# Blocks of tokens behind a branch on their count, in two routed layers

## The chip, the cores and the metric

The kernel runs on one core of one Trainium2 chip (trn2). A core has TensorE for matrix products (its weight loads are shown as an engine of their own, PEld), VectorE (DVE), ScalarE (ACT), GpSimd (POOL) and SyncE (SP), each with an instruction queue of its own, and DMA engines that move data between the chip's main memory and the core's SBUF. TensorE writes into PSUM. The metric is the device time of one execution in microseconds (us); lower is better.

## The reference

One network of four layers runs over 16 batches of 64 tokens with 256 features, x of shape (16, 64, 256), and over a context of 16 x 1024 rows. Each layer is a cross attention, a mixing step and a feed-forward part, each added to x. Two of the feed-forward parts matter here; both are routed: a router gives every token to one or two of eight experts.

```python
# layer 0: two experts of eight per token, and a shared expert
scores = jax.nn.softmax(xt @ gate_w.T, axis=-1)
topk_w, topk_i = jax.lax.top_k(scores, 2)
comb = jnp.zeros((T, E)).at[jnp.arange(T)[:, None], topk_i].add(topk_w)
for e in range(E):
    y = y + comb[:, e:e + 1] * _swiglu(xt, w1[e], w2[e], w3[e])
# layer 1: one expert of eight per token
gates = one_hot(argmax(probs)) * probs
h = relu(einsum('bsd,edf->besf', x, W1) + b1)
y = einsum('besf,efd->besd', h, W2) + b2
out = einsum('bse,besd->bsd', gates, y)
```

There are 1024 tokens, so 2048 assignments in layer 0 and 1024 in layer 1. The hidden width is 704 in layer 0 (`silu(t @ w1) * (t @ w3) @ w2`) and 1024 in layer 1. How many tokens an expert gets is known only once the router has run.

## The kernel before, in words

The kernel computes only the assigned tokens. It writes the normalized tokens to a buffer `hs` in main memory, ranks them within their experts, and cuts every expert's list into blocks of 128. With eight experts, 2048 assignments fill at most 16 + 7 = 23 blocks and 1024 at most 8 + 7 = 15; these are `L0_BLOCKS` and `L1_BLOCKS`. The program always runs that many. A block that is past the last one in use takes the last expert's weights and some of its tokens again; its result is written to rows that nobody reads.

`blocks` (from line 1232 on) makes the tables for it on VectorE: `nb`, the blocks of each expert, `end`, their running sum, and from these, for every block, the rows of the weights (`rows`) and the rows of the tokens (`tokens`). It is a chain of some 25 small operations with one small matrix product in it.

For each block j, GpSimd issues three gathers by indirect DMA (`gather_rows`, line 1280): the first weights into `wa`, the second weights into `wb`, the tokens into `hb`. Each has three buffers, so the gathers run up to three blocks ahead of the products. TensorE transposes the tokens (line 179), VectorE or ScalarE in turn copies them to SBUF as `dT` (`evict`, lines 60 and 62: a switch flips at each call when the program is written out), TensorE multiplies with `wa` into PSUM (`gu` in layer 0, `ph` in layer 1, line 67), ScalarE and VectorE apply the activation and write `hid`, and TensorE multiplies `hid` with `wb` into `po`. ScalarE copies `po` to `yb` (line 1303) and issues its write to the buffer `ys` on its own DMA queue (line 1304). The next layer begins with `carry`, which gathers from `ys` by the tokens' places and adds to x.

In layer 0, `L0_ffn` first runs the second half of the shared expert (`shared_part`, lines 1150 to 1169), which uses a tile `hid` of its own with two buffers, while `blocks` runs and the first gathers are on their way. In layer 1, `L1_ffn` adds the experts' second bias by eight small products in the same place.

The order of the work within a layer is found by a planner of the framework from priorities (the order in which the program is written) and modelled times; it may bring an operation forward past others. Some layers fix TensorE's order by hand; the two routed layers don't. The weights of other layers are brought in by SP into a ring of two slots.

Of the kernel before, what the change touches and what calls it, by code (L numbers as in the profile page):

```python
# [11 lines left out]
F32 = mybir.dt.float32  # L12
I32 = mybir.dt.int32
# [6 lines left out]
B, S, D = 16, 64, 256  # L20
# [4 lines left out]
NK = KEYS // 128  # L25
E = 8
L0_BLOCKS = 2 * T // 128 + E - 1
L1_BLOCKS = T // 128 + E - 1
CAP = 160
L2_CUTS = ((0, 128), (128, CAP - 128))  # L30
RING = 7296
# [5 lines left out]
CHUNK = 256  # L37
# [3 lines left out]
class Net:  # L41
# [1098 lines left out]
            nc.vector.tensor_tensor(g, p, m, ALU.mult)  # L1140
            self.over_experts(g, ALU.add, "", r.gates[x][:, tiles])

    def L0_block(self, j):
        w = self.lp.tile([128, 4 * 704], F32, tag="wa", bufs=3, name="wa")
        self.gather_rows(w, self.a["L0f_w13"], self.rows[:, j : j + 1])
        w2 = self.lp.tile([128, 6 * D], F32, tag="wb", bufs=3, name="wb")
        self.gather_rows(w2, self.a["L0f_w2r"], self.rows[:, j : j + 1])
        return w.rearrange("p (u c f) -> p u c f", u=2, c=2), w2.rearrange("p (m f) -> p m f", f=D)

    def shared_part(self, k):  # L1150

        nc = self.nc
        w1, w3, w2 = self.shared
        cols = bass.ts(k, CHUNK)
        hid = self.lp.tile([128, 3, CHUNK], F32, tag="hid", bufs=2, name="hid")
        for m in range(3):
            at = slice(m * 128, m * 128 + 128)
            ps = self.lps.tile([128, 2, CHUNK], F32, tag=self.tag, bufs=self.tag_bufs, name="gu")
            for u, w in enumerate((w1, w3)):
                self.mm(ps[:, u, :], [(w[:, c, at], self.hT[:, c, cols]) for c in range(2)])  # L1160
            g = self.lp.tile([128, CHUNK], F32, tag="g", bufs=2, name="g")
            nc.scalar.activation(g, ps[:, 0, :], AF.Silu)
            nc.vector.tensor_tensor(hid[:, m, :], g, ps[:, 1, :], ALU.mult)
            yield
        for t in range(2):
            po = self.misc([128, D])
            self.mm(po, [(hid[:, m, t * 128 : (t + 1) * 128], w2[:, m, :]) for m in range(3)])
            self.add_to_x(2 * k + t, po)
            yield

    def L0_ffn(self):
        nc = self.nc
        self.rows, self.tokens = self.blocks(self.routed, L0_BLOCKS)
        self.tag, self.tag_bufs = "gu", 4
        for k in range(2, NC):
            for _ in self.shared_part(k):
                pass
        self.start_pack(self.at)
        sizes = [128] * 5 + [64]
        for j in range(L0_BLOCKS):  # L1180
            w13, w2 = self.L0_block(j)
            dT = self.block_tokens(j)
            hid = self.lp.tile([128, 6, 128], F32, tag="hid1", bufs=2, name="hid1")
            for m2 in range(3):
                ps = self.lps.tile([128, 2, 2, 128], F32, tag="gu", bufs=4, name="gu")
                for v in range(2):
                    m = m2 * 2 + v
                    n = sizes[m]
                    for u in range(2):
                        self.mm(  # L1190
                            ps[:n, u, v, :], [(w13[:, u, c, m * 128 : m * 128 + n], dT[:, c, :]) for c in range(2)]
                        )

                for lo, v, n in ((0, 2, 128),) if m2 < 2 else ((0, 1, 128), (1, 1, 64)):
                    g = self.lp.tile([128, 2, 128], F32, tag="g1", bufs=3, name="g1")
                    nc.scalar.activation(g[:n, :v, :], ps[:n, 0, lo : lo + v, :], AF.Silu)
                    nc.vector.tensor_tensor(
                        hid[:n, m2 * 2 + lo : m2 * 2 + lo + v, :], g[:n, :v, :], ps[:n, 1, lo : lo + v, :], ALU.mult
                    )
            po = self.lps.tile([128, D], F32, tag="o", bufs=2, name="po")  # L1200
            self.mm(po, [(hid[:n, m, :], w2[:n, m, :]) for m, n in enumerate(sizes)])
            self.block_out(j, po)

# [25 lines left out]
    def blocks(self, r, n_blocks):  # L1232


        nc = self.nc
        ps = self.misc([128, E])
        self.mm(ps, [(self.ones, r.seen)])

        nb = self.lp.tile([128, E], F32, name="nb")
        nc.vector.tensor_scalar(nb, ps, 127.0, 1.0 / 128, ALU.add, ALU.mult)  # L1240
        nc.vector.tensor_scalar(nb, nb, 0.49609375, 12582912.0, ALU.subtract, ALU.add)
        nc.vector.tensor_scalar(nb, nb, 12582912.0, None, ALU.subtract)
        end = self.lp.tile([128, E], F32, name="end")
        nc.vector.tensor_tensor_scan(end, self.ones[:, :E], nb, 0.0, ALU.mult, ALU.add)
        shape = [128, n_blocks, E]
        past = self.lp.tile(shape, F32, name="past")
        nc.vector.tensor_tensor(
            past, self.steps[:, :n_blocks].unsqueeze(2).to_broadcast(shape),
            end.unsqueeze(1).to_broadcast(shape), ALU.is_ge,
        )  # L1250
        of = self.lp.tile([128, n_blocks], F32, name="of")
        nc.vector.tensor_reduce(of, past, AX.X, ALU.add)
        nc.vector.tensor_scalar(of, of, E - 1.0, 128.0, ALU.min, ALU.mult)
        rows = self.lp.tile([128, n_blocks], I32, name="rows")
        nc.vector.tensor_scalar(rows, of, self.lane, None, ALU.add)

        nc.vector.tensor_tensor(past, past, end.unsqueeze(1).to_broadcast(shape), ALU.mult)
        at = self.lp.tile([128, n_blocks], F32, name="at_block")
        nc.vector.tensor_reduce(at, past, AX.X, ALU.max)
        nc.vector.tensor_tensor(at, self.steps[:, :n_blocks], at, ALU.subtract)  # L1260
        nc.vector.tensor_scalar(at, at, T / 128 - 1.0, None, ALU.min)
        nc.vector.scalar_tensor_tensor(at, of, T / 128 / 128, at, ALU.mult, ALU.add)
        nc.vector.tensor_scalar(at, at, self.lane, None, ALU.is_equal)
        ps = self.misc([128, n_blocks])
        self.mm(ps, [(r.table, at[: E * T // 128])])
        tokens = self.lp.tile([128, n_blocks], I32, name="tokens")
        nc.vector.tensor_copy(tokens, ps)
        first = self.lp.tile([128, E], F32, name="first")
        nc.vector.tensor_tensor(first, end, nb, ALU.subtract)
        nc.vector.tensor_scalar(first, first, 128.0, 1.0, ALU.mult, ALU.subtract)  # L1270
        for m, to in zip(r.masks, r.at):
            t = self.gate("back_t")
            nc.vector.tensor_tensor(t, r.place, first.unsqueeze(1).to_broadcast([128, NT, E]), ALU.add)
            nc.vector.tensor_tensor(t, t, m, ALU.mult)
            slot, _ = self.over_experts(t, ALU.add, "back_r")
            nc.vector.tensor_copy(to, slot)
        return rows, tokens

    def gather_rows(self, out, src, at):
        return self.nc.gpsimd.indirect_dma_start(out, None, src, bass.IndirectOffsetOnAxis(ap=at, axis=0))  # L1280

# [8 lines left out]
                self.xs[:, i, :], y, g[:, i : i + 1], self.xs[:, i, :], ALU.mult, ALU.add  # L1290
            )

    def block_tokens(self, j):

        hb = self.lp.tile([128, D], F32, tag="hb", bufs=3, name="hb")
        self.gather_rows(hb, self.hs, self.tokens[:, j : j + 1])
        dT = self.lp.tile([128, 2, 128], F32, tag="dT", bufs=2, name="dT")
        self.evict(dT, self.transposed(hb))
        return dT
# [10 lines left out]
        self.nc.sync.dma_start(b2, self.a["L1f_b2"])  # L1310
        return w, row, b2

    def L1_block(self, j):
        w = self.lp.tile([128, 2 * 1024 + 8], F32, tag="wa", bufs=3, name="wa")
        self.gather_rows(w, self.a["L1f_W1b"], self.rows[:, j : j + 1])
        w2 = self.lp.tile([128, 8 * D], F32, tag="wb", bufs=3, name="wb")
        self.gather_rows(w2, self.a["L1f_W2r"], self.rows[:, j : j + 1])
        return (
            w[:, : 2 * 1024].rearrange("p (c f) -> p c f", f=1024), w[:, 2 * 1024 :],
            w2.rearrange("p (m f) -> p m f", f=D),  # L1320
        )

    def L1_ffn(self):
        nc = self.nc
# [9 lines left out]
        for i in range(NT):  # L1334
# [4 lines left out]
            po = self.misc([128, D])  # L1339
            self.mm(po, [(gT, b2)])  # L1340
            self.add_to_x(i, po)
        for j in range(L1_BLOCKS):
            w1, b1, w2 = self.L1_block(j)
            dT = self.block_tokens(j)
            hid = self.lp.tile([128, 8, 128], F32, tag="hid", bufs=2, name="hid")
            for m4 in range(2):
                ph = self.lps.tile([128, 4, 128], F32, tag="h", bufs=3, name="ph")
# [9 lines left out]
            po = self.lps.tile([128, D], F32, tag="o", bufs=2, name="po")  # L1357
            self.mm(po, [(hid[:, m, :], w2[:, m, :]) for m in range(8)])
            self.block_out(j, po)

    def pack_L2_gate(self):
        self.slot()
# [900 lines left out]
```

## Time and profile before

| | us |
|---|---|
| median of 3 runs | 3081.01 |
| lowest and highest run | 3073.53, 3089.68 |
| the profiled execution | 3078.14 |
| its span | 3076.4 |
| blocks of layer 0, first to last result | 301.69 to 503.96 |
| blocks of layer 1, first to last result | 1240.46 to 1347.93 |

The page and the answers of the trace give times from the span's start. A row of the timeline reads: start, duration, engine, line, operation, what it writes and reads, the tile's shape, how many are merged in the row (xN), and in brackets how long the engine had been idle before it and what ended that. A row of the waits reads: who waited for whom, the sum, how many times, the longest. A row of the stretches reads: the stretch, its length, and each engine's busy time with its number of instructions, then the granted TensorE clock, the busy share of the DMA engines and what they moved. The DMA rows read: queue, packets, MB, share of 16 engines' time.

### The profile page before, as it was taken

The page shows a single profiled execution, that of the slowest core. Times are in us where ns is not written, and L with a number is a line of the kernel's source. Part 1 is how long each engine was busy: PE and PEld are TensorE (multiplying, and loading weights), DVE is VectorE, ACT ScalarE, POOL GpSimd, SP SyncE. Part 2 cuts the span into 40 slices and gives each one's busy share as a digit, 9 for nine tenths or more (in the row PEclk, how much of TensorE's full clock was granted, in tenths as well). Part 3 has the DMA queues.
Part 4 walks back from the last instruction along what each step waited for, and adds up shares of the span by engine and source line. Part 5 has one row for each costly group of instructions (what it writes and reads, how often), then busy time and mean ns, then how long its engine had stood idle before and what let it go on. Part 6 is the DMA issues. An engine that isn't in the chain of part 4 may idle for free. (4 is left out here: it accounts for less than half of the span.)

```text
span 3076.4 us, 43295 instructions
## 1 busy us (share of the span) xinstructions
PE 2761.9 (90%) x17200; PEld 2003.3 (65%) x17200; DVE 1495.2 (49%) x3202; ACT 1019.6 (33%) x2187; POOL 324.2 (11%) x440
## 2 busy tenths in 40 slices
PE   7888998999999788979999998896999888887899
PEld 3566886566666445867777776793766666665668
DVE  3554112666666563223444444322445656658591
ACT  1231221455555311223233322121325445445330
POOL 1112332100000011310101001101000000000000
PEclk9997998999999987989999998897999999998999
DMA  9613774101010102831111122461113213122110
GB/s 226 170 37 150 278 277 111 41 25 39 25 35 22 39 4 102 296 116 54 45 52 56 42 59 74 158 221 59 45 47 99 65 43 95 46 72 56 56 35 7
DMA packets 144709, 267.59 MB, mean 87 GB/s; under 512 B 17503, under 2 KB 97723, under 8 KB 137723
## 3 DMA queue, kind: packets, MB, share of 16 engines
q1 hardware_dynamic: 122170, 164.22, 18.4%
q0 software_dynamic: 15328, 94.31, 8.8%
q10 hardware_dynamic: 7008, 6.29, 0.6%
q8 instruction: 135, 2.21, 0.3%
q14 instruction: 68, 0.55, 0.1%
HBM read 247.83 MB, written 14.82 MB: 85 GB/s over the span
## 5 line engine op out<-in xcount | busy, mean ns | idle before, releaser
L223 DVE TENSOR_REDUCE nmx<-sc 128x1 f32<-128x1024 f32 x264 | 311.6, 1218 | 235.2 <-PE sc L498 149.6
L225 ACT ACTIVATE p<-sc,nmx 128x1024 f32<-128x1024 f32 x264 | 294.4, 1116 | 312.5 <-DVE nmx L223 310.8
L498 PE MATMUL sc<-ctxT,qp 128*128 128x512 f32 (+1 forms) x1024 | 354.0, 600 | 0.0
L498 PEld LDWEIGHTS sc<-ctxT,qp 128*128 128x128 f32 (+1 forms) x1024 | 138.5, 189 | 152.9 <-issue 151.4
L67 PE MATMUL halves<-ctx,pT 128*128 128x193 f32 x1024 | 190.2, 340 | 9.1 <-DVE xs L87 4.1
L160 POOL TENSOR_TENSOR ln_rs<-ln_ve,nhalf 128x1 f32<-128x1 f32 x120 | 66.9, 562 | 1194.8 <-DVE ln_ve L158 1085.6
L67 PEld LDWEIGHTS halves<-ctx,pT 128*128 128x128 f32 x1024 | 178.0, 200 | 12.0 <-DVE xs L87 4.6
L67 PE MATMUL misc<-ctx,pT 128*128 128x193 f32 x1024 | 179.2, 327 | 0.4 <-DVE qT L463 0.4
L67 PEld LDWEIGHTS misc<-ctx,pT 128*128 128x128 f32 x1024 | 167.8, 191 | 2.0 <-DVE qT L463 0.8
L235 PE MATMUL ps_t<-ident,p 128*128 128x128 f32 x1088 | 148.2, 278 | 18.1 <-ACT p L225 13.9
L1900 DVE TENSOR_TENSOR_SCAN x<-da,x 128x512 f32<-128x512 f32 x128 | 152.1, 1211 | 2.1 <-ACT da L1890 1.4
L237 ACT COPY pT<-ps_t 128x512 f32<-128x512 f32 x182 | 104.0, 583 | 147.0 <-PE ps_t L235 146.5
L1890 ACT ACTIVATE da<-rep,al 128x252 f32<-128x252 f32 x256 | 114.7, 498 | 114.0 <-DVE x L1900 92.4
L235 PE MATMUL misc<-ident,p 128*128 128x128 f32 x1024 | 138.6, 281 | 14.3 <-ACT p L225 6.7
L235 PEld LDWEIGHTS ps_t<-ident,p 128*128 128x128 f32 x1088 | 127.7, 143 | 32.4 <-ACT p L225 17.2
L235 PEld LDWEIGHTS misc<-ident,p 128*128 128x128 f32 x1024 | 110.7, 141 | 40.7 <-ACT p L225 13.4
L67 PE MATMUL gu<-dT,wa 128*128 128x128 f32 (+1 forms) x1104 | 132.2, 278 | 4.7 <-ACT dT L62 3.1
L67 PEld LDWEIGHTS gu<-dT,wa 128*128 128x128 f32 (+1 forms) x1104 | 123.9, 183 | 13.8 <-ACT dT L62 5.7
L67 PE MATMUL po<-wb,hid 128*128 128x256 f32 x516 | 124.5, 388 | 0.0
L67 PE MATMUL ps_h<-r,w 128*128 128x256 f32 x512 | 115.3, 385 | 0.0
L237 ACT COPY pT<-misc 128x512 f32<-128x512 f32 x128 | 75.1, 586 | 114.4 <-PE misc L235 114.0
L67 PEld LDWEIGHTS ps_h<-r,w 128*128 128x128 f32 x512 | 97.8, 192 | 16.7 <-issue 2.9
(467 smaller groups left out, 4486.3 us busy)
## 6 DMA issues: line engine op xcount, KB each, us to landing
ctx<-in_ctx SPq DMA_DIRECT2D x48, 768.0 KB, 5.0
ctxT<-in_ctxT SPq DMA_DIRECT2D x48, 512.0 KB, 3.3
w<-in_L2f_W SPq DMA_DIRECT2D x24, 1024.0 KB, 7.8
rep<-dus SPq DMA_DIRECT2D x256, 64.0 KB, 2.0
ctxT<-in_ctxT SPq DMA_DIRECT2D x16, 768.0 KB, 13.3
ctxT<-in_ctxT SPq DMA_DIRECT2D x96, 128.0 KB, 3.7
ys<-yb ACTq DMA_DIRECT2D x46, 128.0 KB, 4.0
bc_rep<-bcs SPq DMA_DIRECT2D x32, 128.0 KB, 3.0
```

The costliest lines, as they stand in the source:

```text
L67: self.nc.tensor.matmul(out, lhsT, rhs, start=n == 0, stop=n == len(pairs) - 1)
L160: nc.gpsimd.tensor_tensor(rs, ve, self.nhalf, ALU.pow)
L223: self.nc.vector.tensor_reduce(nmx, sc, AX.X, ALU.max, negate=True)
L225: self.nc.scalar.activation(p, sc, AF.Exp, bias=nmx, accum_out=sums)
L235: self.nc.tensor.transpose(ps[:, u, :], p[:, at : at + 128], self.ident)
L237: self.nc.scalar.copy(pT[:, 4 * g : 4 * g + 4, :], ps)
L498: nc.tensor.matmul(sc[u][:, bass.ts(kh, 512)], qp[n][par][rows, h : h + 2, :].rearrange("p h q -> p (h q)"), ctx[0][rows, at], start=n == ...
L1890: nc.scalar.activation(da[:, g, :, 1:], now[j][:, 0, :].rearrange("p (b s) -> p b s", s=S)[:, :, 1:], AF.Exp, scale=al[:, col : col + 1],)
L1900: nc.vector.tensor_tensor_scan(flat, da.rearrange("p g b s -> p (g b s)"), flat, 0.0, ALU.mult, ALU.add)
```

## The change

The number of blocks in use, `end` of the last expert, is converted to an integer and loaded into a register of every engine. Blocks 18 to 22 of layer 0 and block 14 of layer 1 stand in a conditional arm: it is entered where the count is above 18 or above 14. The arm is placed behind block 3, and blocks 4 to 17 (4 to 13) follow it. Tiles of the arm that gathers fill (`wa`, `wb`, `hb`) have one buffer of their own each, so that they share none with the blocks around it. Ahead of the blocks GpSimd fills a tile with zeros, and SP writes it to the rows of `ys` that belong to the arm. The tile `hid` of the shared part now shares a ring of three buffers with the blocks' `hid1`; before they had two each.

```diff
+L0_FEW = 18
+L1_FEW = 14
...
-    def L0_block(self, j):
-        w = self.lp.tile([128, 4 * 704], F32, tag="wa", bufs=3, name="wa")
+    def L0_block(self, j, own):
+        w = self.lp.tile([128, 4 * 704], F32, tag="wa" + own, bufs=1 if own else 3, name="wa")
...
-        w2 = self.lp.tile([128, 6 * D], F32, tag="wb", bufs=3, name="wb")
+        w2 = self.lp.tile([128, 6 * D], F32, tag="wb" + own, bufs=1 if own else 3, name="wb")
...
-        hid = self.lp.tile([128, 3, CHUNK], F32, tag="hid", bufs=2, name="hid")
+        hid = self.lp.tile([128, 3, CHUNK], F32, tag="hid1", bufs=3, name="hid")
...
-        for j in range(L0_BLOCKS):
-            w13, w2 = self.L0_block(j)
-            dT = self.block_tokens(j)
-            hid = self.lp.tile([128, 6, 128], F32, tag="hid1", bufs=2, name="hid1")
+        def block(j, own=""):
+            w13, w2 = self.L0_block(j, own)
+            dT = self.block_tokens(j, own)
+            hid = self.lp.tile([128, 6, 128], F32, tag="hid1", bufs=3, name="hid1")
...
+        self.some_blocks(block, L0_FEW, L0_BLOCKS)
...
         nc.vector.tensor_tensor_scan(end, self.ones[:, :E], nb, 0.0, ALU.mult, ALU.add)
+        n = self.lp.tile([1, 1], I32, name="n_blocks")
+        nc.vector.tensor_copy(n, end[:1, E - 1 :])
+        self.n_blocks = nc.values_load(n, min_val=0, max_val=n_blocks, skip_runtime_bounds_check_because="counted")
...
+    def some_blocks(self, block, few, most):
+
+        zero = self.lp.tile([128, D], F32, tag="yb", bufs=3, name="zero")
+        self.nc.gpsimd.memset(zero, 0.0)
+        self.nc.sync.dma_start(
+            self.ys[few * 128 : most * 128].rearrange("(n p) d -> p n d", p=128),
+            zero.unsqueeze(1).to_broadcast([128, most - few, D]),
+        )
+        for j in range(4):
+            block(j)
+        with self.tc.If(self.n_blocks > few):
+            for j in range(few, most):
+                block(j, "_few")
+        for j in range(4, few):
+            block(j)
...
-    def block_tokens(self, j):
+    def block_tokens(self, j, own=""):
-        hb = self.lp.tile([128, D], F32, tag="hb", bufs=3, name="hb")
+        hb = self.lp.tile([128, D], F32, tag="hb" + own, bufs=1 if own else 3, name="hb")
```

In layer 1, `L1_block` gets the same `own` argument and the same single buffers, its loop over 15 blocks becomes a function `block(j, own="")`, and `self.some_blocks(block, L1_FEW, L1_BLOCKS)` calls it.

More of the change, by code (lines that the diff above doesn't have):

```diff
@@ L1311, in pack_L1_gate, with L1_block @@
         return w, row, b2
-    def L1_block(self, j):
-        w = self.lp.tile([128, 2 * 1024 + 8], F32, tag="wa", bufs=3, name="wa")
+    def L1_block(self, j, own=""):
+        w = self.lp.tile([128, 2 * 1024 + 8], F32, tag="wa" + own, bufs=1 if own else 3, name="wa")
         self.gather_rows(w, self.a["L1f_W1b"], self.rows[:, j : j + 1])
-        w2 = self.lp.tile([128, 8 * D], F32, tag="wb", bufs=3, name="wb")
+        w2 = self.lp.tile([128, 8 * D], F32, tag="wb" + own, bufs=1 if own else 3, name="wb")
         self.gather_rows(w2, self.a["L1f_W2r"], self.rows[:, j : j + 1])
@@ L1341, in L1_ffn, with block @@
             self.add_to_x(i, po)
-        for j in range(L1_BLOCKS):
-            w1, b1, w2 = self.L1_block(j)
-            dT = self.block_tokens(j)
+        def block(j, own=""):
+            w1, b1, w2 = self.L1_block(j, own)
+            dT = self.block_tokens(j, own)
             hid = self.lp.tile([128, 8, 128], F32, tag="hid", bufs=2, name="hid")
@@ L1359, in L1_ffn @@
             self.block_out(j, po)
+        self.some_blocks(block, L1_FEW, L1_BLOCKS)
     def pack_L2_gate(self):
```

## The prediction

> **What bounds it now.** I read the head of the page first, then the busy time of the engines in stretches of the two stages that the change touches, then the waits inside the first stage, then single rows of the timeline.
>
> ```profile
> span 3076.4 us, 43295 instructions
> PE 2761.9 (90%) x17200; PEld 2003.3 (65%) x17200; DVE 1495.2 (49%) x3202; ACT 1019.6 (33%) x2187; POOL 324.2 (11%) x440
> ...
> q8 instruction: 135, 2.21, 0.3%
> ```
>
> ```profile
> core 0: us, PE busy (x) PEld busy (x) DVE busy (x) ACT busy (x) POOL busy (x), PEclk, DMA share, GB/s
> 281.00:293.00 12.00, 11.32 (x44) 9.01 (x42) 5.11 (x21) 1.15 (x3) 7.81 (x8) 0.81 0.80 317
> ...
> 376.00:422.00 46.00, 45.27 (x314) 38.76 (x312) 8.32 (x23) 9.55 (x28) 15.10 (x16) 1.00 0.76 274
> ```
>
> TensorE is busy 45.27 of 46 us among the blocks of the first routed layer, so a block is worth there what TensorE spends on it. DMA is at 0.76, not the bound. The waits agree: GpSimd's gathers wait for buffers that TensorE frees, never TensorE for weights.
>
> ```profile
> POOL wa L1280 <- PE gu L67: 80.6, 20, 4.8
> ACT yb L1303 <- PE po L67: 47.8, 23, 2.1
> ```
>
> A block ends with the copy of its result (L1303). Its first and last times, with the matmuls that follow it:
>
> ```profile
> 301.69 0.37 ACT L1303 COPY yb<-po 128x256 f32<-128x256 f32 x1 [2.08 <-PE po L67]
> 302.06 0.37 ACT L62 COPY dT<-misc 128x256 f32<-128x256 f32 x1
> 302.12 0.35 ACTq L1304 DMA_DIRECT2D ys<-yb  x1
> 302.49 5.75 PE L67 MATMUL gu<-dT,wa 128*128 128x128 f32 x48 [0.46 <-ACT dT L62]
> ...
> 503.96 0.37 ACT L1303 COPY yb<-po 128x256 f32<-128x256 f32 x1 [2.08 <-PE po L67]
> ```
>
> From 301.69 to 503.96 there are 22 periods: 202.3 us, 9.2 each. The first five take 9.56 to 9.62; later ones alternate 9.56 and 8.66, since transposes for two blocks then share one turn. In the second routed layer the copies run from 1240.46 to 1347.93, 14 periods, 107.5 us: the first five 8.03 to 8.10, then 7.03 and 8.03 in turn.
>
> **Are the arms skipped?** The branch asks for more than 18 and more than 14 blocks. The router's counts, worked out from the reference and its own inputs, are 249, 254, 253, 321, 311, 213, 213, 234 in the first layer: in blocks of 128, 2+2+2+3+3+2+2+2 = 18. In the second: 19, 1, 12, 668, 0, 274, 36, 14, that is 1+1+1+6+0+3+1+1 = 14. Both stand exactly at the limit, so neither arm runs. The nearest edge is the 254: three more tokens there would make 19.
>
> **What is removed.** First layer: 17 periods stay of 22. The three up to block 3 are as before (301.69 to 330.43, 28.7), the next one 9.6 plus the gap of the branch, then 13 more. If these begin unpaired again, as the stage does now, they take 5 x 9.58 + 4 x 18.22 = 120.8; if paired at once 118.9. I take 119.9. Saved: 202.3 - 28.7 - 9.6 - 119.9 = **44.0**. Ends: never paired, 39.5; paired at once, 45. Second layer: 13 stay of 14: 3 x 8.03, one of 8.03, nine more at 68.3 to 70.3, say 69.3; saved 107.5 - 101.4 = **6.0** (5 to 7.5).
>
> **What the branch costs on TensorE.** Nothing of block 4 can be put ahead of it any more, on any engine. No branch is in the trace of before, so I bound it. [...] Three paths lead to block 4's first matmul:
>
> - *TensorE itself.* A block has 62 matmuls and as many weight loads, so five are 620 instructions. The instruction queue of TensorE moved 2.21 MB in 135 packets for 34,400 instructions: 64 bytes each, 255 in a packet, a packet taking 0.3% x 16 x 3076 / 135 = 1.1 us. The arm is 2.4 such packets, [...] By the rows it is a packet (1.1) and the latency of a small transfer (the shortest gather of token rows lands in 2.3): about 3. Without a stall, 0.3. After it come transposes 0.4 and the copy with its hand-overs 0.8, less the 0.8 that stands between two blocks now: **3.4**, ends 0.5 and 7 (a gather's landing when the queues are full, 7.1).
> - *ScalarE.* Block 3's result leaves on ScalarE's own DMA queue; in this stage that lands after 1.7 to 4.0 us, median 3.8. If ScalarE waits for it, it is back 0.4 + 0.35 + 3.8 + 0.3 = 4.9 after the last matmul, and queued behind are the copy of dT and the Silu of block 4. The copies alternate between VectorE and ScalarE; with five in the arm, block 4's falls to ScalarE, and TensorE waits for that one: 4.9 + 1.0 - 0.8 = **5.1**.
> - *GpSimd.* Block 4's gathers are queued behind a wait for block 3's: issued 303.17, landed by about 310, where wa of block 4 was issued at 308.51. About 1.5 late, and not needed before 331: nothing. Had GpSimd to wait for TensorE as well, this is the second rival.
>
> The paths run beside each other: 5.1 in the first layer. In the second the arm is one block, 100 instructions, [...] the results land in 4.6 to 7.2, median 5.9. With dT on VectorE, ScalarE comes back 7 us after the last matmul, when TensorE has done block 4's first product and is waiting for its activations: 2.8 late; with dT on ScalarE 7.0. I take 4.0, ends 1 and 7.
>
> **The clock.** The first block of the second layer, after a thin stretch, beside the next one:
>
> ```profile
> 1231.95 5.01 PE L67 MATMUL ph<-dT,wa 128*128 128x128 f32 x32 [0.46 <-ACT dT L62]
> 1236.80 3.62 PE L67 MATMUL po<-wb,hid 128*128 128x256 f32 x16
> 1240.26 0.38 PE L179 MATMUL misc<-ident,hb 128*128 128x128 f32 x2
> 1241.16 3.84 PE L67 MATMUL ph<-dT,wa 128*128 128x128 f32 x32 [0.52 <-DVE dT L60]
> ```
>
> The same 32 matmuls take 5.01 rather than 3.84, 1.2 more. [...] Today the stage has gaps of 0.8 and a clock of 1.00. [...] by the row 1.2. [...] **1.2 and 0.5**.
>
> **What is added ahead.** The count's copy (a VectorE operation of 0.17 as those beside it) stands in the chain that makes the gather's rows, and a register load on each engine waits for it. On TensorE the shared part is queued behind it, on ScalarE its Silu, on SP the 292 us weight loads for the next layer, on GpSimd the zero fill and the first gather; the four had been idle by then. On VectorE `past` and so the first gather come later by the copy and the load, 0.6 as an estimate from three such small operations. The zero write (five blocks of 128 KB, 0.64 MB, at the stage's 317 GB/s 2.1 us) goes out on SP just before the first gathers and shares their engines; block 0's rows land at 290.7 and are used at 291.7, so 1 us covers it, and of 2.7 I let **1.0** through (0 to 2). Second layer: 0.13 MB, and the bias products cover the gathers till 1230.8; the chain itself is 0.6 longer, **0.8** with the write. The arm's own buffers (15 KB a partition more, after the shared `hid` tag) may move tiles of the next layer onto ones still in use: covered, since the next layer begins with work in PSUM; 0 to 4 without that cover. The third `hid` buffer saves nothing where TensorE is full.
>
> **Sum.** First layer 44.0 - 5.1 - 1.2 - 1.0 = 36.7; second 6.0 - 4.0 - 0.5 - 0.8 = 0.7. Gain 37.4 on the profiled execution's 3078.1 (its span 3076.4 and 1.7 around it): 3040.7. The median of the runs shown is 2.9 higher: **3043**.
>
> **Rivals.**
> 1. *The branch is nearly free* (0.15): waits on results in flight are not needed, the fetch is hidden by queued matmuls. Then 50 - 2 x 1.0 - 1.8 = 46 are gained: 3035. For it: GpSimd and SP are far ahead. Against: TensorE itself has no slack.
> 2. *The branch is a full stop for the gathers* (0.19): GpSimd passes only when TensorE has finished block 3, and block 4's three gathers start from nothing, as at the stage's beginning: first gather 281.38, first product about 293, 11.5 us, less 0.8, in each layer. 50 - 21.4 - 1.7 - 1.8 = 25: 3056. [...] Against: GpSimd's gathers have buffers of their own in the arm.
> 3. *The arm of the first layer runs* (0.04), the one that ends slower: 19 blocks counted on the chip. Nothing is saved there; in the arm one buffer per kind lets a weight gather start only when the block before is through with it: 0.9 to issue and 7.1 to land against the 3.8 that lie between, 4.2 x 4 = 17, and a gap at entry and at exit, 10: about 3081 + 27 + 1.0 - 0.7 = 3108. It is decided by three tokens at the second expert, and the counts speak against it.
>
> **How the numbers follow.** My forecast has 0.62. Its own range, from the ends above: 3030 to 3055. With rivals 1 and 2 at their ends and the runs' own spread (3073.5 to 3089.7), 8 in 10 lie in 3024 to 3062. Half a per cent of 3081 is 15.4 us, about what a measurement can tell from no change: faster means under 3065.6. All of my case and rival 1, and all but 0.03 of rival 2 are there: faster 0.93, same 0.03, slower 0.04.
>
> **What will show it.** Right: 18 and 14 copies L1303; between the fourth and fifth copy of the first layer some 16 us instead of 9.6, with dT on ScalarE as what TensorE waited for, and no GpSimd row in it; the clock under 1.00 just after. Wrong: 23 and 15 copies (rival 3), gathers of block 4 issued after the fourth copy (rival 2), a gap as today (rival 1), or a later layer that starts late for want of room.

## The result and the profile after

| | before | after |
|---|---|---|
| median, us (4 runs each) | 3078.77 | 3039.10 |
| lowest and highest run | 3073.53, 3089.68 | 3038.35, 3043.64 |
| profiled execution, its span | 3078.14, 3076.4 | 3043.64, 3041.8 |
| layer 0, first to last result | 202.27 (23 results) | 163.32 (18) |
| layer 1, first to last result | 107.47 (15) | 101.46 (14) |

The ratio of after to before is 0.987, with a 95% interval of 0.984 to 0.9899: 1.3% faster, 39.7 us by the medians. The forecast was 3043. The total fits better than the steps that lead to it: the wait behind the branch was another one than forecast, and what was put too low in one place met what was put too high in others, as the trace shows.

The head of the page of the kernel after, as it was shown of the kernel before (busy us, share of the span, number of instructions; for the queue packets, MB and share):

```profile
span 3041.8 us, 42516 instructions
...
PE 2714.3 (89%) x16840; PEld 1959.1 (64%) x16840; DVE 1485.3 (49%) x3177; ACT 1006.5 (33%) x2154; POOL 307.5 (10%) x424
...
q8 instruction: 134, 2.20, 0.3%
```

360 matmuls are gone: five blocks of 62 and one of 50. TensorE is busy 47.6 us less and the span is 34.6 us shorter, so in this execution some 13 us of the gain came back as idle time. The stretches of layer 0 show where (three blocks, then the period with the branch, then the other blocks):

```profile
core 0: us, PE busy (x) PEld busy (x) DVE busy (x) ACT busy (x) POOL busy (x), PEclk, DMA share, GB/s
311.60:340.30 28.70, 27.26 (x186) 23.00 (x186) 4.65 (x13) 5.75 (x17) 8.47 (x9) 1.00 0.83 299
340.30:356.90 16.60, 11.13 (x66) 9.59 (x65) 1.83 (x5) 2.06 (x6) 4.73 (x5) 0.79 0.49 168
356.90:474.90 118.00, 116.53 (x804) 99.93 (x804) 21.06 (x61) 24.13 (x71) 29.43 (x35) 1.00 0.68 232
```

The first and the last stretch look like the kernel before: TensorE busy all but 1.5 us, clock 1.00. The middle one holds one block's work in 16.60 us, with a clock of 0.79. Its rows in the timeline, with the results at the stage's beginning and end around them:

```profile
311.60 0.37 ACT L1326 COPY yb<-po 128x256 f32<-128x256 f32 x1 [2.08 <-PE po L69]
...
340.34 0.37 ACT L1326 COPY yb<-po 128x256 f32<-128x256 f32 x1 [2.08 <-PE po L69]
340.74 0.33 ACTq L1327 DMA_DIRECT2D ys<-yb  x1
345.68 1.09 PE L181 MATMUL misc<-ident,hb 128*128 128x128 f32 x4 [5.38 <-PEq L1296]
346.43 0.37 ACT L64 COPY dT<-misc 128x256 f32<-128x256 f32 x1 [5.72 <-PE misc L181]
346.82 0.94 POOL L1303 DMA_INDIRECT wb<-in_L0f_w2r,rows  x1 [8.29 <-PE misc L181]
346.86 7.05 PE L69 MATMUL gu<-dT,wa 128*128 128x128 f32 x48
356.92 0.37 ACT L1326 COPY yb<-po 128x256 f32<-128x256 f32 x1 [2.08 <-PE po L69]
...
474.92 0.37 ACT L1326 COPY yb<-po 128x256 f32<-128x256 f32 x1 [2.08 <-PE po L69]
```

Between the fourth and the fifth result lie 16.58 us, 7.0 more than the 9.56 that a block takes there. TensorE was idle 5.38 of it, and what ended that is its own sequencer at L1296, the `If`; the profile names no other engine. ScalarE had issued block 3's result at 340.74 and then sat idle for 5.72 until TensorE's transposes came, so the wait runs the other way round from the forecast's. The rest is clock: the 48 matmuls into `gu` take 7.05 us instead of the 5.75 of before, and the four transposes (of two blocks in one turn) 1.09, where four take 0.66 at full clock in the kernel with a hint, further down.

The rows of line L1296 and the register load (engine or its queue, operation, number; shortest, median and longest in ns; first and last start in us; one each per layer):

```profile
L1296 POOLq EVENT_SEMAPHORE  x5: 17/43/7058, 338.1 to 1237.6; - x5
...
L1296 DVEq COMPARE_BRANCH  x2: 63/68/72, 338.9 to 1236.6; - x2
L1296 PEldq COMPARE_BRANCH  x2: 225/3187/6149, 339.2 to 1237.0; - x2
...
L1296 ACTq COMPARE_BRANCH  x2: 45/45/45, 341.6 to 1238.8; - x2
...
L1296 POOLq INC_SWDGE_SEM  x2: 563/1252/1942, 345.5 to 1237.7; - x2
...
L1251 PEldq TENSOR_LOAD <-n_blocks x2: 311/401/491, 338.6 to 1236.6; - x2
```

TensorE's compare-and-branch takes 6149 ns in layer 0 and 225 in layer 1. The same instruction takes 45 to 72 on ScalarE and VectorE. The instruction queue q8 moves one packet in the wait (DMA row of the stretch 339.3 to 345.3):

```profile
q8 instruction: 1, 0.02, 1.1%
```

It starts 3.65 us after the branch and takes 1.07; TensorE goes on 1.43 after its end. The next packet follows 6.82 us after the branch, just as the stage goes on. That q8 is TensorE's is an inference: among the blocks of layer 0 in the kernel before its packets start 17.8 to 19.3 us apart, which is two blocks of TensorE's work, and its 2.20 MB here are 65 bytes for each of the 33,680 matmuls and weight loads.

GpSimd stood 7.06 us at a semaphore, from 338.1 on; that it is one of its own gathers is read from their packets, the last of which starts at 344.79. Behind it its next gather came at 346.82. The gathers of blocks 4 and 5 had gone out before, and no product waited for it. In layer 1 the period with the branch is 8.52 us and the next one 8.62, against about 8.0: one microsecond in all (in a second trace of this kernel 8.52 and 8.03, so half of one). The results at the two ends of that period, in the timeline:

```profile
1238.43 0.37 ACT L1326 COPY yb<-po 128x256 f32<-128x256 f32 x1 [2.30 <-PE po L69]
...
1246.95 0.37 ACT L1326 COPY yb<-po 128x256 f32<-128x256 f32 x1 [2.30 <-PE po L69]
```

### The profile page after: what moved, and what is told of

It is laid out like the page before. It is cut to its first block, busy times and chain, and to the rows that moved or that the text cites. A ratio compares the mean times of both kernels' runs of the same rounds, so it can differ in the third digit from the quotient of the medians.

```text
span 3041.8 us, 42516 instructions
## 1 busy us (share of the span) xinstructions
PE 2714.3 (89%) x16840; PEld 1959.1 (64%) x16840; DVE 1485.3 (49%) x3177; ACT 1006.5 (33%) x2154; POOL 307.5 (10%) x424
## 4 chain that ended last, share of the span: by engine, by line
PE 65%; DVE 11%; ACT 4%; DMA 3%; issue 3%; POOL 1%; SPq 1%; ACTq 0%; DVEq 0%; POOLq 0%
PE misc L69 11%; PE sc L500 8%; PE halves L69 7%; PE gu L69 5%; PE misc L237 4%; PE po L69 4%; PE ps_h L69 4%; PE ps_t L237 3%; PE sc L69 2%; PE misc L863 2%; PE o L914 2%; PE misc L877 2%; PE ph L69 2%; DVE x L1925 2%; DMA back<-ys,route_at 2%
## 5 line engine op out<-in xcount | busy, mean ns | idle before, releaser
L225 DVE TENSOR_REDUCE nmx<-sc 128x1 f32<-128x1024 f32 x264 | 311.7, 1218 | 242.2 <-PE sc L500 147.9
L69 PE MATMUL gu<-dT,wa 128*128 128x128 f32 (+1 forms) x864 | 104.8, 280 | 4.1 <-ACT dT L64 1.9
L241 DVE COPY pT<-misc 128x512 f32<-128x512 f32 x128 | 88.2, 689 | 38.8 <-PE misc L237 28.3
L69 PE MATMUL po<-wb,hid 128*128 128x256 f32 (+1 forms) x440 | 105.9, 388 | 0.3 <-ACT hid L1379 0.3
```

The costliest lines, as they stand in the source:

```text
L69: self.nc.tensor.matmul(out, lhsT, rhs, start=n == 0, stop=n == len(pairs) - 1)
L225: self.nc.vector.tensor_reduce(nmx, sc, AX.X, ALU.max, negate=True)
L241: self.nc.vector.tensor_copy(pT[:, 0:4, :], ps)
```

## The experiments

Theories for the gap of layer 0 that these two traces leave standing: TensorE has to fetch code from beyond the arm (A in the expectations: a short arm is jumped over cheaply, and the price does not grow with every block of a long one); a fixed price of any branch (B: the same for an arm of one block); a price in proportion to the length (F: 3/5 of it for three blocks); and hand-overs behind the arm, ScalarE's or GpSimd's. Besides, how much is lost outside of the blocks. All these kernels compute the whole output.

### No branch

```diff
-        n = self.lp.tile([1, 1], I32, name="n_blocks")
-        nc.vector.tensor_copy(n, end[:1, E - 1 :])
-        self.n_blocks = nc.values_load(n, ...)
...
-        for j in range(4):
-            block(j)
-        with self.tc.If(self.n_blocks > few):
-            for j in range(few, most):
-                block(j, "_few")
-        for j in range(4, few):
+        for j in range(few):
             block(j)
```

> 18 blocks in the first layer and 14 in the second, always, with no count loaded and no branch; the zero write and the shared hid ring stay. Theory A (the branch of the first layer costs 7.0 us because TensorE has to fetch code it has jumped to, that of the second 0.5): all the rest of the gain is the blocks that are gone, so this is 7 to 9 us faster than the changed kernel, about 3031, with 9.6 or 8.7 between the fourth and fifth result instead of 16.6. Theory B (the gap is what it costs to start the gathers and products again with single-block pairing lost): the gap shrinks only in part, 3034 to 3038.

Measured: median 3045.11 us (3041.16 to 3047.33), ratio 0.9883 (0.9867 to 0.99). Layer 0 took 157.16 us, its fourth to fifth result 9.62, and layer 1 100.8. So in the blocks the branch costs 6.2 us in layer 0 and 0.7 in layer 1, and the blocks that are gone are worth 202.27 - 157.16 = 45.1 and 6.7. But the kernel as a whole was not faster than the one with the branch: the expected 3031 was missed by 14 us. Everything outside the two stretches of blocks took 2783.3 us, against 2766.6 in the kernel before. Once more, beside the kernel after:

> The kernel without a branch, 18 and 14 blocks, beside them. Its blocks took 6.2 us less than the changed kernel's in the profiles (157.2 against 163.3 in the first layer, 100.8 against 101.5 in the second), yet its runs took 6 us more. Theory C (what lies outside the blocks differs from run to run or from chip to chip): 3033 to 3036 here, below the changed kernel. Theory E (the planner lays out something else in it that costs about 12 us in every run): 3041 to 3047 again, above the changed kernel.

Measured: 3041.19 us (3036.83 to 3043.95), ratio 0.9868 (0.9848 to 0.9888); blocks 157.17 and 100.43, outside 2783.9. It is the same again. Without the branch the blocks are 7 us shorter than in the kernel after, and the rest is longer by 6 to 10 (2777.0 and 2773.7 there); the section on the forecast comes back to this.

### The length of the arm

```diff
-L0_FEW = 18
+L0_FEW = 22
```

> The arm of the first layer holds one block (22) instead of five; blocks 18 to 21 run unconditionally. 124 TensorE instructions are jumped over instead of 620. Theory A (code fetch): TensorE's compare-and-branch takes about 0.2 us instead of 6.15, and the fourth and fifth result lie about 10.1 apart. Theory B (the cost is in letting every engine finish and raising the semaphores, whatever the arm's length): about 6 us again, 16.6 apart.

With 21 and 20 in the place of 22 the arm has two and three blocks:

> The first layer's arm holds two blocks (21 and 22), 248 TensorE instructions, [...] blocks 18 to 20 run unconditionally. Theory A [...]: TensorE's branch takes 0.2 to 0.4 us [...] or some 6 [...]. Theory B (fixed price): the 0.36 us that the arm of one block showed.

> The first layer's arm holds three blocks (20 to 22), 372 TensorE instructions, [...] blocks 18 and 19 run unconditionally. Theory A: [...] the branch takes about 6 us and the gap behind block 3 is about 16.6, as with five. Theory F (the wait grows with the length jumped over): about 3.6 us, three fifths of it.

Measured, one run each: 3061.94, 3063.96 and 3054.08 us. The branch's row of each trace (the longest of the two is layer 0's), with an arm of one block:

```profile
L1296 PEldq COMPARE_BRANCH  x2: 219/288/358, 329.8 to 1256.6; - x2
```

With two blocks:

```profile
L1296 PEldq COMPARE_BRANCH  x2: 219/288/358, 338.9 to 1258.1; - x2
```

With three blocks:

```profile
L1296 PEldq COMPARE_BRANCH  x2: 225/3287/6349, 332.1 to 1248.3; - x2
```

An arm of one or two blocks (124 or 248 instructions of TensorE) is jumped over in 0.36 us. Three blocks (372) cost 6.35, and five (620) cost 6.15 and, in a second trace, 6.59. So the price of the branch is neither fixed nor in proportion to the length; it is a step between 248 and 372 instructions. The gap of layer 0 was 0.4 us with one block, 2.1 with two and 7.3 with three.

With two blocks most of the gap is not in the branch. TensorE stands still in the midst of block 4's products, and no engine ends that wait:

```profile
345.04 3.63 PE L69 MATMUL gu<-dT,wa 128*128 128x128 f32 x29 [1.45 <-issue]
```

A packet of its instruction queue starts 3.85 us after this branch too, takes 0.90, and 6.14 us after the branch TensorE goes on, as it does 6.15 after the branch over five blocks. So it looks like the same stall of some 6.1 us, met some 55 instructions behind the branch, whose work covered the greater part of it. What a jump costs then does not depend on its length alone. Why those 55 ran ahead of the stall with 248 jumped over, and none with 372, no trace shows. In these traces TensorE began some 185 to 200 instructions between the last packet ahead of the branch and the branch itself; where the step lies for a branch at another place was not measured.

### Telling the fetch beforehand

The kernel is unchanged but for a hint in TensorE's program, placed behind block 2, that the coming branch is likely taken:

```diff
-        for j in range(4):
+        for j in range(3):
             block(j)
-        with self.tc.If(self.n_blocks > few):
+        label = f"few{few}"
+        if few == L0_FEW:
+            self.tc.mark_branch_hint_location(label, "LikelyTaken", [mybir.EngineType.PE])
+        block(3)
+        with self.tc.If(self.n_blocks > few, label=label if few == L0_FEW else None):
```

> The changed kernel with a prefetch hint to TensorE for the branch of the first layer (the planner puts the hint at the start of the program). Theory A: if the hint makes TensorE fetch the target ahead, the branch takes 0.2 to 1 us and the kernel is 5 to 7 us faster than the changed one, about 3033; if a hint so far ahead does nothing, 3039 as the changed kernel. Theory B: 3039 in either case.

Measured: 3031.59 us (3029.28 to 3033.47), ratio 0.9839 (0.9823 to 0.9856), the fastest kernel here. The branch's row in this kernel:

```profile
L1300 PEldq COMPARE_BRANCH  x2: 235/314/393, 329.4 to 1220.5; - x2
```

What follows it in the timeline, up to the fifth result:

```profile
332.10 0.66 PE L181 MATMUL misc<-ident,hb 128*128 128x128 f32 x4 [1.59 <-ACTq L1300]
333.05 7.38 PE L69 MATMUL gu<-dT,wa 128*128 128x128 f32 x48 [0.30 <-ACT dT L64]
...
343.45 0.37 ACT L1330 COPY yb<-po 128x256 f32<-128x256 f32 x1 [2.08 <-PE po L69]
```

The same jump over the same five blocks takes 0.39 us instead of 6.15. Nothing else on TensorE's way was changed, so the hint took 5.76 us of stall away. The planner had moved it to the start of the program (0.8 us into the span), and it worked from there. That the stall is a fetch of code is the reading that fits: from the branch to the fifth result TensorE's queue moves one packet here and two in the kernel after, while the last one ahead of the branch comes some 14 us before it in both. What a packet holds no trace shows.

The gap shrank from 7.0 to 3.3 us. The next in line is ScalarE, whose skip ended the 1.59 that TensorE still waits, and behind that comes a stretch at a granted clock of 0.50 (7.38 instead of 5.75 for the 48 matmuls):

```profile
329.70:333.10 3.40, 1.51 (x8) 0.77 (x7) 0.31 (x1) 0.74 (x2) 0.00 (x0) 1.00 0.84 338
333.20:336.40 3.20, 3.20 (x16) 3.20 (x17) 0.01 (x1) 0.00 (x0) 0.00 (x0) 0.50 0.25 85
```

Once more, beside the kernel after:

> The changed kernel with the hint, beside it. Theory A (code fetch): faster than the changed kernel by the 3.7 us that the gap between the fourth and fifth result shrank in its first profile (16.6 to 12.9), 3 to 7 us in all. Theory B: no difference.

> The changed kernel once more, on the same chip and in the same rounds as the next two. In its first profile the stretch ahead of the first layer's blocks took 9.9 us longer than before. Theory C (that stretch, which loads the context and runs at a clock that comes and goes, differs from run to run): the first result now comes at 301 to 307 and not at 311.6; the branch of the first layer again takes 6 us on TensorE, and its gap is 16 to 17. Theory D (the shared hid ring or the moved tiles cost it in every run): the first result again at 310 or later.

Measured: with the hint 3034.22 us (3033.19 to 3045.94), ratio 0.9862 (0.9836 to 0.9888); the changed kernel 3037.88 (3036.67 to 3040.19), ratio 0.986 (0.9843 to 0.9877). Layer 0 takes 159.63 and 159.64 us in the two traces of the hint, 163.32 and 163.74 without: 3.7 and 4.1 us are there. Of the whole, the medians give 7.5 and 3.7. The first of these compares runs of different rounds, and in both the intervals of the ratios overlap, so that the total alone does not show the gain; the stage does.

### One branch per block

```diff
-        for j in range(4):
-            block(j)
-        with self.tc.If(self.n_blocks > few):
-            for j in range(few, most):
-                block(j, "_few")
-        for j in range(4, few):
+        for j in range(few):
             block(j)
+            if 3 <= j < 3 + most - few:
+                with self.tc.If(self.n_blocks > few + j - 3):
+                    block(few + j - 3, "_few")
```

> The five blocks of the first layer stand in five arms of one block each, behind blocks 3, 4, 5, 6 and 7; each is skipped on its own count. Theory A: [...] each branch costs the 0.5 us that the second layer's one costs, and about 0.45 for transposes that can't be paired across it: 5 x 0.95 = 4.8 instead of 7.0, about 3037. Theory B: every branch costs 6 to 7 us, 28 more than the changed kernel, about 3067.

Measured: 3038.97 us (3036.57 to 3046.41), ratio 0.9871 (0.9853 to 0.9889). Line L1297 here is the five branches of layer 0 and the one of layer 1:

```profile
L1297 PEldq COMPARE_BRANCH  x6: 219/376/432, 332.1 to 1226.5; - x6
```

Five short jumps cost some 0.4 us each where one long one costs 6.15; the periods with a branch are 9.9 to 9.99 us instead of 9.56, so hardly more than the branch itself is lost in them. Layer 0 takes 159.93 us, as with the hint. The median of the whole is no lower than the kernel after's (3039.10 and 3037.88), so the total does not show this gain.

### The arm is entered

```diff
-        with self.tc.If(self.n_blocks > few):
+        with self.tc.If(self.n_blocks > few - (few == L0_FEW)):
```

> The first layer's branch asks for more than 17, so with 18 blocks in use its arm runs: 23 blocks there, as before; the second layer is as changed. The third rival of the prediction put this at 3108: 17 us because the arm's single buffers hold back each weight gather until the block before is through with it, and 10 for gaps at entry and exit. Theory A adds that the arm lies next in TensorE's code, so that no fetch is waited for at entry: its branch takes 0.2 to 0.4 us and the whole 3095 to 3108.

Measured, one run: 3106.21 us, 23 results in layer 0 in 240.52 us. The periods around the arm are 22.39, 14.56, 15.94, 14.87, 15.86 and 10.17. TensorE's timeline in the first two of these periods:

```profile
343.92 0.69 PE L181 MATMUL misc<-ident,hb 128*128 128x128 f32 x2 [9.88 <-DMA hb<-hs,tokens]
345.12 8.33 PE L69 MATMUL gu<-dT,wa 128*128 128x128 f32 x48 [0.51 <-DVE dT L62]
...
360.66 7.35 PE L69 MATMUL gu<-dT,wa 128*128 128x128 f32 x48 [3.86 <-DMA wa<-in_L0f_w,rows]
```

At the entry TensorE waits 9.88 us for the arm's first token gather. Inside, a weight gather that can start only when the one buffer is free keeps it 3.86. The 48 matmuls behind these waits take 8.33 and 7.35 instead of 5.75. This is the third rival's mechanism: 12.8 at the entry, 23 more over the four periods that follow (61.2 against 4 x 9.56), 0.6 at the exit, while the branch falls through in 0.08. Its 17 and 10 were thus 23 and 13.4. That the total still meets its 3108 is luck: outside of the blocks this one run took 2762.2 us, against 2766.6 before, and layer 1 gave back 5.9.

### The branch ahead of the shared part

In the kernel with the hint, the `If` was moved to the front; the shared part (in layer 1 the bias products) and all blocks follow it:

```diff
-        for j in range(4):
-            block(j)
-        with self.tc.If(self.n_blocks > few):
...
+        with self.tc.If(self.n_blocks > few, label=label if few == L0_FEW else None):
             for j in range(few, most):
                 block(j, "_few")
-        for j in range(4, few):
+        rest()
+        for j in range(few):
             block(j)
```

> The hinted kernel with both branches moved to the start of their layers: the arm stands ahead of the shared part (first layer) and of the bias products (second), and all blocks follow. Theory A for TensorE: its branch takes 0.4 us where it was waiting anyway, and no gap is left behind block 3 (9.6). GpSimd lets its own gathers land before it raises their semaphores (7.06 us in the changed kernel, hidden there because it was three blocks ahead): the planner leaves one gather of block 0 ahead of the branch, so the others start some 7 us late, the first result of the first layer comes 5 to 8 us later, and the whole is 3 to 6 us slower than with the hint behind block 3. If GpSimd's wait were hidden here too, 3 us faster.

Measured, one run: 3047.46 us, 13 to 16 more than with the hint behind block 3, where 3 to 6 were expected. Layer 0's blocks are at their shortest, 155.86 us, but the first result comes 33.0 us after `end` is known, not 23.4 or 23.1 as in the two traces of the hint. The gathers say why:

```profile
280.04 1.22 POOL L1307 DMA_INDIRECT wa<-in_L0f_w,rows  x1 [16.30 <-DVE at_block L1271]
288.96 0.94 POOL L1307 DMA_INDIRECT wb<-in_L0f_w2r,rows  x1 [7.70 <-remote]
```

Block 0's first gather is issued ahead of GpSimd's skip, and the second goes only after 7.70 us of idle time, about what such a gather takes to land (7.1 and 8.2 us for the first two into `wa` in the kernel before): the skip is taken to have waited for it. Behind block 3 the same wait is there (7.06) and costs nothing, since the gathers of the next two blocks have gone out. Here there are none, and it costs 9.6 to 9.9 us. This is about what the second rival put at 10.7, gathers that start from nothing, though GpSimd waits here for its own gather and not for TensorE. Less the 3.8 won in the blocks it makes the 6 that were expected; the other 8 to 11 us fall elsewhere outside of the blocks, in a run with more time at half clock (378.9 us against 344.7), and why is open.

### The kernel before again

> The kernel before once more, for its profile. Theory C (what lies outside the blocks differs from run to run): the blocks take 202.3 and 107.5 again within 0.5 us, and what lies outside them, 2766.6 us in its first profile, differs by some us.

Measured, one run: 3081.43 us; layer 0 202.27, layer 1 107.92, outside 2769.5 us. The stages repeat within 0.5 us; the rest of the kernel moved by 2.9.

## Why the forecast was right, and where not

**The removal** was sized as 44.0 and 6.0; by the kernel without a branch it is 45.1 and 6.7. Behind the branch the blocks were paired at once (periods of 8.66 from the first on): the 13 take 118.0 us, a little below the better of the two ends, 118.9. (Small slips stand in the working: the fifth period of before is 9.47 and not 9.56 or more, the terms of the 44.0 as written give 44.1, and 3040.7 + 2.9 is 3043.6.)

**The gap of the branch in layer 0** is the step that failed in its mechanism. The forecast let ScalarE decide, with 5.1 us for a result's landing, and put TensorE's own fetch behind it: about 3 for the fetch, 3.4 with what follows. ScalarE did not wait for the landing at all: its branch started at 341.64, less than a microsecond after it issued the write, and took 0.045; the packets of that write moved from 343.2 to 345.2. Without the landing ScalarE's path is what the kernel with the hint shows, where TensorE waits 1.59 us for it. SP, which had nothing to do then, passed semaphores of the skipped arm from 311.7 on. The stall is 6.15, twice the estimate for a fetch, which was built from one packet (1.1, measured 1.07) and one small transfer's latency (2.3): the trace has 3.65 us before the packet even starts and 1.43 behind it. What fills these two no run shows. So 5.1 (by ScalarE) became 5.38 of idle time (by TensorE): close by luck, because one term was too small and the other did not exist. That a jump over five blocks stalls at all was an assumption of the forecast, which no row of before showed; here it does, for 6.15 us. That it sets in between 248 and 372 instructions, and that with 248 a part of it comes 55 instructions later, is what the arms of two and three blocks show.

**The clock.** 1.2 was put in for layer 0. In the kernel after 6.8 us ran at half rate, beginning 2.5 us after TensorE had come to rest:

```profile
340.30:342.80 2.50, 0.01 (x1) 0.00 (x0) 0.00 (x0) 0.37 (x1) 0.00 (x0) 1.00 0.96 406
342.80:349.60 6.80, 3.83 (x17) 3.46 (x18) 0.42 (x1) 0.37 (x1) 2.17 (x3) 0.50 0.29 85
```

The 48 matmuls lost 1.3 and the four transposes 0.4, so the step was right in kind and the size 1.7. For layer 1 0.5 was put in, and no half-clock time is there (granted clock 1.00 from 1230.4 to 1305.0). From which length an idle time costs clock was the author's estimate, which no row of before showed. In the kernel with the hint the idle times were shorter: TensorE was busy for 1.51 of 3.40 us at a clock of 1.00, its longest idle time there 1.59, and a stretch at 0.50 followed (its rows from 329.70 and 333.20, further up), which cost the 48 matmuls 1.6. The 1.45 us of idle time in the kernel with an arm of two blocks were not followed by one (granted clock 1.00). What sets it off, and whether the idle time alone does, no run here separates.

**The gap in layer 1** was taken as 4.0, from the landing of the results. It is 1.0, over two periods (0.5 in the second trace, 0.7 by the kernel without a branch), for the same reason as above: the landing was nobody's wait. Of a term of 4.0, 3.0 were not there.

**The setup ahead** was 1.0 and 0.8; from `end` to the first product it is 0.4 and 0.2 more than before, and in layer 0 two traces of one kernel differ by as much. The register loads do not stand ahead of the layer's work, as the forecast had it: the planner put each right before its engine's branch, TensorE's at 338.6. The zero write was issued at 275.1, long before the first gather at 290.9, so nothing of it met the gathers.

**GpSimd.** "Nothing of block 4 can be put ahead of it any more, on any engine" is wrong there: the gathers of blocks 4 and 5 and one of 6 went out ahead of its branch. The conclusion, nothing lost, held, with this as its cover; with the cover gone it is the 9.6 to 9.9 us of the moved branch.

**The sum.** In the blocks and ahead of them the change gained 44.4 us in the first traces, where the forecast's sum had 37.4:

| us | forecast | measured |
|---|---|---|
| blocks that are gone, layers 0 and 1 | 44.0 + 6.0 | 45.1 + 6.7 |
| gap and clock, layer 0 | 5.1 + 1.2 | 6.2 |
| gap and clock, layer 1 | 4.0 + 0.5 | 0.7 |
| setup, layers 0 and 1 | 1.0 + 0.8 | 0.4 + 0.2 |
| gain (measured: from the unrounded terms) | 37.4 | 44.4 |

The 6.2 of layer 0 are 7.0 in the one period, less 0.8 that the pairing behind it gave back. By the medians the kernel gained 39.7, and 43.0 when both were run again: some of the 44.4 was lost again outside of the blocks, which the forecast had at nothing. So that the total came within 4 us is in part luck: a sum that was 7 us too small met a loss that was not in it. In the first trace of after the loss begins at 38 us, where nothing of the change is near:

```profile
38.57 5.35 PE L332 MATMUL sc<-ctxT,qp 96*64 96x512 f32 x14 [3.36 <-DMA ctxT<-in_ctxT]
```

That wait did not come again in the second trace (first result at 304.2 instead of 311.6, the kernel before 301.7 and 305.4), and the second trace of the kernel before has one of 1.87 at the same place. Time outside of the blocks goes with the clock. The mean granted clock and the time of all 49 executions of the ten kernels, fitted with one slope and a level for each kernel, give 1.9 us for 0.001 of clock, and leave 2.4 us. At a clock of 0.942 the levels are 3082.9 before, 3037.4 after, 3034.7 with the hint and 3037.7 without a branch. At an equal clock the change is worth 45.5, near what the blocks say (44.4). The fit is a description and shows no cause: the mean clock also falls because the blocks that are gone ran at full rate, by somewhat under 0.001 as an estimate from the 355 us at half rate of the kernel before.

**What stays open** is the kernel without a branch. By its blocks it should beat the one with the hint by 3 us, and it was 7 to 13.5 slower. TensorE ran 368.6 and 378.9 us of its two traces at half rate, against 344.7 in both of the hint, some 3.3 of which stand in the gap behind the branch (twice the 1.63 that the 48 matmuls lost there). Half of the difference that is left, 14 to 19 us, is as an estimate what that costs where TensorE is the bound, and the parts outside of the blocks were longer by 13 to 16, of which 8 to 9 lie behind layer 1's last result. So the half-clock time is enough in size, but that it is the cause is argued and not shown: at an equal clock the fit still has this kernel 3 us above the one with the hint. Why the clock falls so in that program, in both rounds, was not found out by any run.

## What to carry to other kernels

Before code is put behind a branch on an engine that has no slack, count that engine's instructions in the arm: 124 were jumped over in 0.4 us here, 248 cost 1.5 more a little later, and from 372 on it took 6.2 to 6.6. Either several short arms or a branch hint took this price away in the stage; the whole kernel's medians were 4 to 7 us lower with the hint, with intervals that overlap, and no lower with the short arms. Put the branch where the engine that issues the gathers is blocks ahead, since its skip waited for what it had in flight: 7.06 us that were free behind block 3, and 7.70 that were nearly 10 us of the kernel's time ahead of block 0. An arm with single buffers and a cold entry is dear when entered (36 us for five blocks here), so the count that decides it has to be far from the limit or nearly certain.

## What the runs showed of the hardware that was not expected

- The jump's price is a step (0.36 us at 124 and 248 instructions of TensorE, 6.35 at 372, 6.15 and 6.59 at 620), and 3.65 us of it pass before a packet of its queue begins. At 248 TensorE stands idle 1.45 us some 55 instructions later and goes on 6.14 us after the branch.
- A branch hint at the start of the program, some 329 us ahead of the branch, still brought the jump to 0.39 us.
- ScalarE skips an arm in 0.045 us while its own write is in flight; GpSimd waits for its gathers (7.06 us) and then takes another 0.56 for their semaphores (1.94 in layer 1, row INC_SWDGE_SEM).
- In the kernel with the hint 3.40 us in which TensorE was busy for 1.51, with no idle time above 1.59, were followed by a stretch at a granted clock of 0.50 (3.20 of 3.20 us in the row).
- The kernel without a branch and the one with branch and hint differ by 27 to 38 us in the time that TensorE runs at half clock outside of that gap.
